# Two layers of attention and quantized feed-forward on one core: the weights' norm factors, the opening and the order of layer 1's attentions rearranged

## The chip, the core and the metric

The kernel runs on one core of a Trainium2 chip. The metric is the device time of one execution in microseconds (us). The engines have these names in the profile: PE (TensorE, matmuls; PEld is its weight load), DVE (VectorE), ACT (ScalarE), POOL (GpSimd), SP (SyncE, which here only issues DMAs).

## What is computed

Eight sequences of 512 tokens with 256 features (B = 8, T = 512, C = 256), each with a context of 512 x 128, 16 heads. Two layers; each adds a gated attention and a gated feed-forward to x:

```python
x = x + tanh(g_xattn[0]) * L0_xattn(layernorm(x), ctx)   # head size 16
x = x + tanh(g_ffn[0])   * L0_ffn(layernorm(x))
x = x + tanh(g_xattn[1]) * L1_xattn(layernorm(x), ctx)   # head size 32
x = x + tanh(g_ffn[1])   * L1_ffn(layernorm(x))

# L0_xattn: causal self-attention plus full cross-attention, one projection
y = softmax(causal(q k')) v + softmax(qc kc') vc;  return y @ Wp + bp
# L0_ffn: both linears on values quantized with ONE scale for all tokens
#   scale = (max(x) - min(x)) / 255, before W1 and, after gelu, before W2
# L1_xattn: two blocks, a1 on (x, x) and a2 on (x, ctx); each block:
xn, yn = ln(x, lnx_g, lnx_b), ln(y, lny_g, lny_b)
a = softmax((xn wq)(yn wk)' / sqrt(32))     # a1: then a *= (t > s)
x_out = x + (a (yn wv)) @ li1 + li1_b
out = x_out + gelu(ln(x_out) @ li2 + li2_b) @ li3 + li3_b
# L1_ffn: ternary weights, activations in 8 bits with a scale per token
h = silu(depthwise_conv1d(bit_linear(x, w1), 3 taps));  return bit_linear(h, w2)
```

The global minimum and maximum after gelu in L0_ffn mean that no second linear of layer 0 can start before the last token's gelu is done. That splits the kernel into two parts.

## The kernel before

A planner at build time (`Pace`) holds a modelled free time for each engine and a modelled ready time for each tile. Work is written as Python generators, *streams*. `weave_timed` (layer 0 and the stage between the layers) and `weave_all` (layer 1) choose, step by step, which stream goes next, and thereby write out the instruction order of every engine; nothing is reordered at run time. A stream yields `need(...)`, the tiles that its next step reads, or `WAIT`. A stream has a base (from which attention on it may run) and a share of the time. All matmuls are issued by `mm` (line 1050) and all transposes by `tp` (line 1053), so rows of PE bear these two lines.

Layer 0, for each sequence b: `norm0` (layer norm), `pre0` (transposes to xnT through `turned_timed`, then `values0`), `pairs0` (the projections Q and K of a half of the heads, self and cross), `cross0` (the cross values), `steps0` (the attention itself: scores into a tile of two PSUM banks, two exponentials, GpSimd's causal mask on the diagonal, then the output matmuls into `ov`), `post0`. PSUM holds three score tiles of two banks (`st`), one bank `ov` and one bank for everything else (`m0`, `bank()`), so that in layer 0 every projection, transpose and value product passes through one bank in turn. Before the first attention stands a chain of norm0(0), pre0(0) and pairs0(0, 0, 0). The weights of layer 1 are loaded and prepared by `load1` beside layer 0's attentions: block a1's during b = 5, a2's during b = 6. Preparing a weight is to multiply the norm's factor into it (line 1542, DVE) and to work the norm's bias through it into a bias of its own (16 small matmuls, or 4 for the values of a1, and a small DVE operation, lines 1529 and 1539).

Between the layers, `layer0_ffn`: `range0(b)` quantizes, multiplies by W1, applies gelu, takes minimum and maximum (tile `hext`, line 1665) and stores the result to DRAM (hd). `keys2` makes the context's keys and values for the first six sequences. Then two reduces into `e` (lines 1589 and 1590) and a chain of small operations give the scale of the second quantization. The PSUM pool here has eight single banks.

Layer 1, `layer1_xattn`: 16 attentions (8 sequences x 2 blocks), each a *slot*, in the order of a list `order`. Slots go in rows: two sequences in a1, the same two in a2, the next two in a1 and so on. The weights li1, li2, li3 of a block are held once, so they are loaded anew for each row: `used` starts the next load when the last sequence of a row has used them, `weight` waits for it. Beside the attentions run these streams:

- `first(b)`: second half of layer 0's feed-forward: loads h (tile hF), on ACT scales and rounds it (line 1912), on DVE clips (1914) and subtracts (1916), and multiplies by W2, in two halves of 256 tokens;
- `pre1`, `pair1`: layer norms, transposes, Q and K of a group of four heads;
- `mlp1(b, blk, half)`: li1, li2, gelu, li3; in its first half for a2 it also loads the sequence's values vt from DRAM;
- `last(b)`: layer 1's feed-forward: the convolution on DVE (line 2290), silu on ACT, the maximum of |h| over 1024 features for each token (hm, line 2298, a reduce), a multiply by the token's scale and the rounding into hq (2315), and the product with w2;
- `tail` for the last sequence, `diagonals`, `keys2_rest`.

An attention slot is four groups of four steps. A step's front is four score matmuls, two exponentials of 128 x 1024 (line 2175) and for a1 the masked diagonal `dg` by GpSimd (line 2179). Its back is the output matmuls and, over the four steps, sums on DVE (lines 2204 and 2206, tile acc); at a group's end ones-matmuls, two DVE transposes, a reciprocal and a multiply (line 2224) give oT and free the one bank of `ov`. PSUM in layer 1: two score tiles of two banks, one bank `ov`, three for the rest.

Of the kernel before, what the change touches and what calls it, by code (L numbers as in the profile page):

```python
# [15 lines left out]
P = 128  # L16
B, T, C, CC = 8, 512, 256, 128
H = 16
NT = T // P
# [7 lines left out]
NEG = -1.0e30  # L27
PTS = 3
# [886 lines left out]
def need(*tiles, pe=True, room=()):  # L915


    return [Pace.name(t) for t in tiles], pe, room
# [30 lines left out]
class Fast(General):  # L949
# [114 lines left out]
    def weave_timed(self, ops, streams, drain=False):  # L1064

        pace, behind = self.pace, self.behind
        ops = list(ops)
        n_ops, i = len(ops), 0  # L1070
        live = list(streams)

        def advance(s):
            w = pace.work
            s.need = next(s.gen, None)
            s.done += pace.work - w
            if s.need is None:
                s.over = True
                if s in live:
                    live.remove(s)  # L1080

        def starts(s):
            names, on_pe, room = s.need
            t = max([pace.when(names)] + [pace.place(tag) for tag in room])
            return max(t, pace.place("m1")) if on_pe else t

        while i < n_ops or live or (drain and not behind.over):
            now = pace.free.get("PE", 0.0)
            cands = []
            for s in live + ([] if behind.over else [behind]):  # L1090
                while s.need is WAIT:
                    last = s.need
                    advance(s)
                    if s.need is WAIT:
                        break
                while not s.over and s.need is not WAIT and not s.need[1] and starts(s) <= now:
                    advance(s)
                if s.over or s.need is WAIT:
                    continue
                cands.append((s.base + s.share * s.done / s.total, starts(s), s))  # L1100
            if i < n_ops:
                cands.append((i / n_ops, ops[i][0](), None))
            if not cands:
                continue
            can = [c for c in cands if c[1] <= now + 0.3]
            pick = min(can, key=lambda c: c[0]) if can else min(cands, key=lambda c: (c[1], c[0]))
            if pick[2] is not None:
                advance(pick[2])
            else:
                ops[i][1]()  # L1110
                i += 1
# [47 lines left out]
    def layer0_xattn(self, w8pool):  # L1159
# [4 lines left out]
        with (  # L1164
# [9 lines left out]
            self.weave_timed([], [Stream(self.chain(self.norm0(0), self.pre0(0), self.pairs0(0, 0, 0)), 1.0)])  # L1174
            for b in range(B):
                streams = [Stream(self.pairs0(b, 1), 7.0, 0.88)]
                if b:
                    streams.append(Stream(self.post0(b - 1), 4.0, 0.88))
                else:
                    streams.insert(0, Stream(self.cross0(0), 5.0, 2.0))  # L1180
                if 1 <= b <= 4:
                    n = ("f0_w1", "f0_w2", "f1_w1", "f1_w2")[b - 1]
                    pool = w8pool if n == "f0_w1" else stage
                    streams.append(Stream(self.few_bits(n, n[1] == "1", pool), 1.0, 0.88))
                if b in (5, 6):
                    streams.append(Stream(self.load1(b - 5), 4.0, 0.88))
                if b + 1 < B:
                    streams.append(Stream(self.norm0(b + 1), 1.0, 0.88))
                streams.append(Stream(self.ctx0(b), 1.0, 0.88))
                self.weave_timed(self.steps0(b, 0), streams)  # L1190
                streams = []
                if b + 1 < B:
                    gen = self.chain(self.pre0(b + 1), self.pairs0(b + 1, 0, 0), self.cross0(b + 1))
                    streams.append(Stream(gen, 14.0, 0.88))
                self.weave_timed(self.steps0(b, 1), streams)
# [154 lines left out]

    def cross0(self, b):
# [18 lines left out]
    def pairs0(self, b, u, *which):  # L1370
# [5 lines left out]
        for s in which or (0, 1):  # L1376
            src = (q["xnT"], q["ctxT"])[s]
            yield need(q["xnT"])
            ps = self.proj(self.wqk[("wq", "wcq")[s]], q["xnT"], u * P)
# [3 lines left out]
            ps = self.proj(self.wqk[("wk", "wck")[s]], src, u * P)  # L1383
# [5 lines left out]
    def steps0(self, b, u):  # L1389
# [7 lines left out]
        def front_at(e, s):  # L1397
            if (u, s) not in q or ("v", s) not in q:
                return 1e9
# [3 lines left out]
        def front(e, s, kt):  # L1403
# [15 lines left out]
            reads = [Pace.name(pt), Pace.name(q["v", s])]  # L1419
            self.coming = (reads, kt == 0, lambda: back(e, s, kt, lo, pt))  # L1420
# [36 lines left out]
        def rest_at():  # L1457
            if self.rest is None:
                return 0.0
            names, opens, _ = self.rest  # L1460
# [40 lines left out]
    def load1(self, blk):  # L1501
# [12 lines left out]
        w = {}  # L1514
        for name, nch, ln in (("wq", 2, "lnx"), ("wk", nchy, "lny"), ("wv", nchy, "lny")):
# [4 lines left out]
            yield need(t)  # L1520
            ps = self.bank()
            if name == "wv" and not blk:
                for c in range(nch):
                    self.mm(
                        ps, self.col(f"{pre}_{ln}_b", c).to_broadcast([P, P]), t[:, c, :],
                        c == 0, c == nch - 1,
                    )
                bias = home.tile([P, 2 * C], F32, name=f"{pre}_{name}_b")
                nc.vector.tensor_copy(bias, ps)
            else:  # L1530
                for g in range(4):
                    for c in range(nch):
                        self.mm(
                            ps[:, g : g + 1], t[:, c, g * P : (g + 1) * P],
                            self.col(f"{pre}_{ln}_b", c), c == 0, c == nch - 1,
                        )
                bias = self.keep2.tile([P, 4], F32, name=f"{pre}_{name}_b")
                s = 32.0 ** -0.5 if name == "wq" else 1.0
                nc.vector.tensor_scalar(bias, ps[:, 0:4], s, None, ALU.mult)
            w[name + "_b"] = bias  # L1540
            for c in range(nch):
                nc.vector.tensor_scalar(
                    t[:, c, :], t[:, c, :], self.col(f"{pre}_{ln}_g", c), None, ALU.mult
                )
        self.w1s.append(w)
        if blk:
# [13 lines left out]
            for p in ("a1", "a2"):  # L1560
                d = self.row1v(f"{p}_li3_b")
                nc.vector.tensor_tensor(d, d, self.row1v(f"{p}_li1_b"), ALU.subtract)

# [4 lines left out]
    def layer0_ffn(self):  # L1568
        nc, tc, small = self.nc, self.tc, self.small
        with (  # L1570
# [10 lines left out]
            for b in range(2):  # L1581
                self.load_cT(b)
            streams = [Stream(self.chain(self.post0(B - 1), self.scales0()), 4.0, 0.01)]
            for b in range(B):
# [152 lines left out]
    def layer1_xattn(self):  # L1737
        nc, tc = self.nc, self.tc
        with (
# [19 lines left out]
            order = [(2 * p + k, blk) for p in range(B // 2) for blk in range(2) for k in range(2)]  # L1759
            few, pairs, mlps, pres = [], [], [[], []], [[], []]  # L1760

            for k, b in zip((-1, 0, 1, 2, 3, 4, 7, 8), range(B)):
# [3 lines left out]
            for k, b in zip((5, 6, 9, 10, 13, 14, 15), range(B - 1)):  # L1766
# [9 lines left out]
            for half in range(2):  # L1776
                mlps[half][-1].base += 0.4 * half
                mlps[half].append(Stream(self.tail(half), 20.0, 1.0, 17 + 0.4 * half))
            self.final, self.tails = {}, [0, 0]
# [4 lines left out]
                [self.steps1(b, blk) for b, blk in order], [few, pairs, *mlps, *pres, diag, keys]  # L1784
# [6 lines left out]
    def weave_all(self, attns, chains):  # L1791
# [14 lines left out]
        def starts(s):  # L1806
            names, on_pe, _ = s.need
            t = max(pace.when(names), pace.free["DVE"] - s.lag)
# [43 lines left out]
    def weight(self, name, b, blk):  # L1852

        while self.loads.get(name) != self.slot_of(b, blk) // 2:
# [3 lines left out]
    def used(self, name, b, blk):  # L1858

        if self.both(b, (name, blk)) and b % 2 and (b, blk) != (B - 1, 1):  # L1860
# [24 lines left out]
    def first(self, b):  # L1885
# [22 lines left out]
        for half in range(2):  # L1908
            if half:
                h = h2 or load_h(1)  # L1910
            yield need(h, pe=False)
            nc.scalar.activation(h, h, AF.Identity, scale=self.rh, bias=self.magic)
            yield need(h, pe=False)
            nc.vector.tensor_scalar(h, h, self.hlo, self.hhi, ALU.max, ALU.min)
            hq = work.tile([P, NF, n], BF16, tag="hq", name="hq")
            nc.vector.tensor_scalar(hq, h, MAGIC, None, ALU.subtract)
# [111 lines left out]
    def slot_of(self, b, blk):  # L2028

        return 4 * (b // 2) + 2 * blk + b % 2  # L2030
# [9 lines left out]
    def pair1(self, b, blk, g):  # L2040
# [17 lines left out]
        self.pairs += 1  # L2058

    def mlp1(self, b, blk, half):  # L2060
# [43 lines left out]
        elif not half:  # L2104
            while self.nvt < self.slot_of(b, 1) or self.backs < 16 * (self.slot_of(b, 1) - 1):
                yield WAIT
            vt = q["vt", 1] = work.tile([P, NT, 2 * C], F32, tag="vt", name="vt", bufs=2)
            self.nvt += 1
            nc.sync.dma_start(vt.rearrange("p t c -> p (t c)"), self.vd[b])
# [134 lines left out]
    def last(self, b):  # L2244
# [25 lines left out]
        for half in range(2):  # L2270
# [3 lines left out]
            for f in range(NF):  # L2274
# [18 lines left out]
            yield need(h, pe=False)  # L2293
            nc.scalar.activation(h, h, AF.Silu)
            yield need(h, pe=False)

            hm = work.tile([P, n], F32, tag="hm", name="hm")
            nc.vector.tensor_reduce(  # L2298
                hm, h.rearrange("p f t -> p t f"), AX.X, ALU.max, apply_absolute_value=True
            )  # L2300
# [11 lines left out]
            yield need(sr, pe=False)  # L2312
            nc.vector.tensor_tensor(h, h, sr.unsqueeze(1).to_broadcast([P, NF, n]), ALU.mult)
            hq = work.tile([P, NF, n], BF16, tag="hq", name="hq")
            nc.vector.tensor_scalar(hq, h, MAGIC, MAGIC, ALU.add, ALU.subtract)
# [239 lines left out]
```

## Time and profile before

| | |
|---|---|
| time, median of 3 runs | 2823.27 us (2820.88 to 2829.08) |
| profiled execution, its own time | 2823.82 us |
| its span | 2822.1 us |
| mean granted TensorE clock | 0.956 |
| PE busy | 2520.0 us (89%) |
| DVE busy | 1725.1 us (61%) |
| ACT busy | 1448.3 us (51%) |
| POOL busy | 615.0 us (22%) |

The span is the profiled execution from its first to its last instruction. Busy times of the engines overlap, and the engine that is busy most is not the only one that sets the end: what counts is what PE waits for, where it waits. "x <- y" in a row of waits means that an instruction on tile x waited for an instruction on tile y. The line numbers are those of the kernel before.

### The profile page before, as it was taken

Reading aid. Unit: us, or ns where it says so; the run is one execution under the profiler, and the core shown is the slowest. Engines: PE = TensorE matmul, PEld = TensorE weight load, DVE = VectorE, ACT = ScalarE, POOL = GpSimd, SP = SyncE. Lnnn points to the kernel's source line nnn. Section 1 sums busy time; section 2 is a strip of 40 time slices with the busy share of each in tenths; the row PEclk is TensorE's granted clock in tenths of the full one; section 3 lists DMA queues with packets and bytes.
Section 4 is the critical chain, followed back from the end, with each engine's and each line's share of the span. In section 5 each row is a group of like instructions: output and inputs, shape, how many; then the busy total and the mean of one; then the engine's idle time right before and its main releaser. Section 6 shows DMA issues by size and latency. Waiting matters only on the chain.

```text
span 2822.1 us, 38446 instructions
## 1 busy us (share of the span) xinstructions
PE 2520.0 (89%) x15452; PEld 1222.3 (43%) x15452; DVE 1725.1 (61%) x3072; ACT 1448.3 (51%) x1785; POOL 615.0 (22%) x682
## 2 busy tenths in 40 slices
PE   6999999999675888999999998999999999898875
PEld 2333333333232334535554445456354455354454
DVE  4544544343475555575657767766767755768766
ACT  4666675666573444445445534454555454555431
POOL 2112222111101343231422121232223112212010
PEclk9999999999897989999999999999999999999988
DMA  3001110010364411312210120131120020121010
GB/s 111 22 29 49 49 64 27 12 34 12 116 272 178 154 45 64 113 64 75 72 53 23 45 90 24 59 131 50 53 90 31 28 78 23 31 83 46 15 45 16
DMA packets 77339, 181.79 MB, mean 64 GB/s; under 512 B 7520, under 2 KB 36576, under 8 KB 69344
## 3 DMA queue, kind: packets, MB, share of 16 engines
q1 hardware_dynamic: 74768, 176.05, 17.9%
q8 instruction: 123, 2.02, 0.3%
q0 software_dynamic: 800, 2.62, 0.3%
q10 hardware_dynamic: 1584, 0.58, 0.1%
q14 instruction: 64, 0.52, 0.1%
HBM read 116.32 MB, written 62.91 MB: 64 GB/s over the span
## 4 chain that ended last, share of the span: by engine, by line
PE 69%; DVE 17%; ACT 7%; issue 3%; POOL 3%; DMA 1%; ACTq 0%; POOLq 0%; DVEq 0%
PE ps L1050 39%; PE ps_s L1050 16%; PE ov L1050 12%; DVE hext L1665 2%; PE ps L1053 2%; POOL dg L2179 1%; ACT pt L1412 1%; ACT pt L2175 1%; DVE hF L2290 1%; DVE hm L2298 1%; DVE acc L2204 1%; DVE mv L1936 1%; DVE acc L2206 1%; DVE rb L2222 1%; ACT hD L2122 1%
## 5 line engine op out<-in xcount | busy, mean ns | idle before, releaser
L2175 ACT ACTIVATE pt<-ps_s 128x1024 f32<-128x1024 f32 x512 | 496.3, 1021 | 443.5 <-PE ps_s L1050 357.1
L1050 PE MATMUL ps_s<-QT,KT 32*128 32x512 f32 (+3 forms) x4096 | 613.2, 610 | 29.0 <-ACT pt L2175 12.6
L1412 ACT ACTIVATE pt<-ps_s 128x1024 f32<-128x1024 f32 (+3 forms) x512 | 411.2, 862 | 197.4 <-PE ps_s L1050 190.9
L1050 PEld LDWEIGHTS ps_s<-QT,KT 32*128 32x128 f32 x4096 | 192.5, 185 | 365.2 <-issue 204.4
L2179 POOL TENSOR_SCALAR_AFFINE_SELECT dg<-pt 128x512 f32<-128x512 f32 x128 | 123.2, 964 | 651.6 <-ACT pt L2175 651.5
L1050 PE MATMUL ps<-li,hD 128*128 128x256 f32 x1024 | 238.8, 389 | 12.1 <-ACT hD L2122 12.1
L1050 PE MATMUL ps<-x3T,li 128*128 128x256 f32 x1024 | 244.0, 390 | 1.4 <-ACT x3T L2092 1.1
L1050 PE MATMUL ov<-pt,v 128*32 128x512 f32 (+3 forms) x2048 | 232.7, 525 | 13.9 <-POOL pt L1415 12.5
L1050 PE MATMUL ov<-pt,vt 128*32 128x512 f32 (+3 forms) x1792 | 204.9, 524 | 39.4 <-DVE oT L2224 33.2
L1050 PEld LDWEIGHTS ps<-li,hD 128*128 128x128 f32 x1024 | 193.4, 193 | 66.2 <-issue 17.6
L1050 PEld LDWEIGHTS ps<-x3T,li 128*128 128x128 f32 x1024 | 192.1, 194 | 55.3 <-issue 15.3
L1415 POOL TENSOR_SCALAR_AFFINE_SELECT pt<-pt 128x512 f32<-128x512 f32 x128 | 87.0, 681 | 477.4 <-ACT pt L1412 477.4
L1942 POOL TENSOR_SCALAR mv<-mv 128x2 f32<-128x2 f32 (+1 forms) x105 | 49.8, 475 | 630.8 <-DVE mv L1937 589.8
L2206 DVE TENSOR_TENSOR acc<-acc,pt 128x2048 f32<-128x2048 f32 x64 | 151.4, 2366 | 8.2 <-ACT pt L2175 7.2
L2204 DVE TENSOR_TENSOR acc<-pt 128x2048 f32<-128x2048 f32 x64 | 149.9, 2342 | 0.6 <-ACT pt L2175 0.6
L1437 DVE STREAM_TRANSPOSE ot<-ov 128x512 f32<-128x512 f32 x64 | 45.8, 716 | 156.3 <-PE ov L1050 156.3
L1050 PE MATMUL ps<-zT,a_wq 128*128 128x512 f32 x256 | 131.7, 640 | 6.1 <-DVE zT L2023 4.1
L2290 DVE SCALAR_TENSOR_TENSOR hF<-hp,cols,hF 128x256 f32<-128x256 f32 x224 | 113.1, 505 | 34.6 <-ACT hF L2281 28.1
L1050 PE MATMUL ps<-li,oT 128*128 128x256 f32 x512 | 128.0, 394 | 1.6 <-DVE oT L2224 1.1
L1050 PEld LDWEIGHTS ps<-li,oT 128*128 128x128 f32 x512 | 94.0, 193 | 44.5 <-issue 16.4
L1050 PEld LDWEIGHTS ov<-pt,v 128*32 128x32 f32 x2048 | 40.5, 107 | 168.0 <-issue 102.2
L1729 ACT ACTIVATE hD<-ps,cols 128x256 f32<-128x256 f32 x121 | 53.7, 472 | 108.8 <-PE ps L1050 72.9
(293 smaller groups left out, 3624.1 us busy)
## 6 DMA issues: line engine op xcount, KB each, us to landing
hd<-h SPq DMA_DIRECT2D x16, 1024.0 KB, 3.9
hF<-hd SPq DMA_DIRECT2D x16, 1024.0 KB, 6.7
li<-in_w_a_dram SPq DMA_DIRECT2D x16, 1024.0 KB, 5.0
fw<-q_f_w SPq DMA_DIRECT2D x22, 512.0 KB, 6.0
xF<-xd SPq DMA_DIRECT2D x22, 512.0 KB, 4.5
kd<-k SPq DMA_DIRECT2D x8, 1024.0 KB, 5.6
vd<-v SPq DMA_DIRECT2D x8, 1024.0 KB, 5.3
res<-rd SPq DMA_DIRECT2D x32, 256.0 KB, 2.7
```

Of the source, the lines that this page charges most:

```text
L1050: self.nc.tensor.matmul(out, lhsT, rhs, start=start, stop=stop, skip_group_check=True)
L1053: self.nc.tensor.transpose(out, in_, self.ident)
L1412: nc.scalar.activation(pt[:, 2 * jp : 2 * jp + 2, lo:], pss[jp][:, :, lo:], AF.Exp)
L1415: nc.gpsimd.affine_select(out=diag, in_=diag, compare_op=ALU.is_ge, fill=0.0, base=0, pattern=[[0, 4], [1, P]], channel_multiplier=-1,)
L1665: nc.vector.tensor_reduce(e, hh, AX.X, op)
L1729: self.nc.scalar.activation(out, ps, AF.Identity, bias=bias)
L1942: nc.gpsimd.tensor_scalar(rstd, mv[:, :, 1], EPS, None, ALU.add)
L2175: nc.scalar.activation(pt[:, 2 * jp : 2 * jp + 2, :], pss[jp], AF.Exp)
L2179: nc.gpsimd.affine_select(out=dg, in_=pt[:, :, diag], compare_op=ALU.is_gt, fill=0.0, base=0, pattern=[[0, 4], [-1, P]], channel_multiplier=1,
L2204: nc.vector.tensor_tensor(st["acc"], st["pt"], pt, ALU.add)
L2206: nc.vector.tensor_tensor(st["acc"], st["acc"], pt, ALU.add)
L2290: nc.vector.scalar_tensor_tensor(a, hp[:, half + k : half + k + n], self.col("conv_w", 3 * f + k), a, ALU.mult, ALU.add)
```

## The change

Four things are changed; the matmuls are the same, in number and shape.

**Opening.** A new `opening0` takes the place of `pre0` and the first `pairs0` for b = 0. All eight transposes go into one score tile of two banks; ACT copies one bank out, DVE the other. Q and K are then projected into the two banks of a second score tile. The values' product moves behind, into a stream beside the first attention, ahead of `cross0`. Fronts of an attention no longer require the values, backs do.

**Norm factors.** The preparation of a1's wq, wk, wv and of a2's wq moves out of `load1` into a new `gains1`, which runs as the stream of the lowest priority in the stage between the layers. Their loads, and all of a2's wk and wv, stay where they were.

**Rows.** Layer 1's attentions go in rows of two, three and three sequences instead of four rows of two. The places from which `first` and `last` may start are shifted to suit, `li` weights are loaded 18 times instead of 24, and the load of vt becomes a stream of its own.

**Halves.** In `first`, the ACT operation and the DVE operations work in two halves of the features. In `last`, the reduce hm goes in two halves of the tokens, and multiply and rounding in two halves of the features. Steps whose first instruction is on ACT are timed by ACT's modelled free time.

```diff
+ROWS = ((0, 1), (2, 3, 4), (5, 6, 7))
+FIRST_AT = (-1, 0, 1, 2, 4, 5, 7, 9)
+LAST_AT = (6, 7, 8, 11, 12, 13, 15)
...
-            self.weave_timed([], [Stream(self.chain(self.norm0(0), self.pre0(0), self.pairs0(0, 0, 0)), 1.0)])
+            self.weave_timed([], [Stream(self.chain(self.norm0(0), self.opening0()), 1.0)])
...
-                    streams.insert(0, Stream(self.cross0(0), 5.0, 2.0))
+                    values = self.values0(0, 0, self.seqs[0]["xnT"], self.wv0["wv"], "bv")
+                    streams.insert(0, Stream(self.chain(values, self.cross0(0)), 12.0, 1.2))
...
+    def opening0(self):
+        q = self.seqs[0]
+        xnT = q["xnT"] = self.work.tile([P, 2, T], F32, tag="xnT", name="xnT", bufs=1)
+        yield need(q["z"], pe=False)
+        ps = self.st.tile([P, 2, T], F32, tag="st", name="ps_s")
+        for c in range(2):
+            for i in range(NT):
+                self.tp(ps[:, c, i * P : (i + 1) * P], q["z"][:, i, c * P : (c + 1) * P])
+        self.nc.scalar.copy(xnT[:, 0, :], ps[:, 0, :])
+        self.nc.vector.tensor_copy(xnT[:, 1, :], ps[:, 1, :])
+        yield from self.pairs0(0, 0, 0, two=True)
...
-            if (u, s) not in q or ("v", s) not in q:
+            if (u, s) not in q:
...
+            n = 2 * C if name == "wv" and not blk else 4
+            w[name + "_b"] = self.keep2.tile([P, n], F32, name=f"{pre}_{name}_b")
+            if home is self.w8pool:
+                yield from self.gains1(blk, name, ln)
...
+            gains = [self.gains1(0, "wq", "lnx"), self.gains1(0, "wk", "lny"), self.gains1(0, "wv", "lny"), self.gains1(1, "wq", "lnx")]
             streams = [Stream(self.chain(self.post0(B - 1), self.scales0()), 4.0, 0.01)]
+            streams.append(Stream(self.chain(*gains), 12.0, 1.0, B))
...
-            order = [(2 * p + k, blk) for p in range(B // 2) for blk in range(2) for k in range(2)]
+            self.rows = [(blk, bs) for bs in ROWS for blk in range(2)]
+            order = self.order = [(b, blk) for blk, bs in self.rows for b in bs]
...
-            for k, b in zip((-1, 0, 1, 2, 3, 4, 7, 8), range(B)):
+            for k, b in zip(FIRST_AT, range(B)):
...
-            for k, b in zip((5, 6, 9, 10, 13, 14, 15), range(B - 1)):
+            for k, b in zip(LAST_AT, range(B - 1)):
...
+            vals = [Stream(self.values2(b), 1.0) for b, blk in order if blk]
...
-            t = max(pace.when(names), pace.free["DVE"] - s.lag)
+            t = max(pace.when(names), pace.free[on] - s.lag)
...
-            yield need(h, pe=False)
-            nc.scalar.activation(h, h, AF.Identity, scale=self.rh, bias=self.magic)
-            yield need(h, pe=False)
-            nc.vector.tensor_scalar(h, h, self.hlo, self.hhi, ALU.max, ALU.min)
+            for f in (slice(0, NF // 2), slice(NF // 2, NF)):
+                yield need(h, pe=False, on="Activation")
+                nc.scalar.activation(h[:, f, :], h[:, f, :], AF.Identity, scale=self.rh, bias=self.magic)
             hq = work.tile([P, NF, n], BF16, tag="hq", name="hq")
-            nc.vector.tensor_scalar(hq, h, MAGIC, None, ALU.subtract)
+            for f in (slice(0, NF // 2), slice(NF // 2, NF)):
+                yield need(h, pe=False)
+                nc.vector.tensor_scalar(h[:, f, :], h[:, f, :], self.hlo, self.hhi, ALU.max, ALU.min)
+                nc.vector.tensor_scalar(hq[:, f, :], h[:, f, :], MAGIC, None, ALU.subtract)
...
-            nc.vector.tensor_reduce(
-                hm, h.rearrange("p f t -> p t f"), AX.X, ALU.max, apply_absolute_value=True
-            )
+            for i in range(2):
+                yield need(h, pe=False)
+                t2 = slice(i * P, (i + 1) * P)
+                nc.vector.tensor_reduce(
+                    hm[:, t2], h[:, :, t2].rearrange("p f t -> p t f"), AX.X, ALU.max, apply_absolute_value=True
+                )
...
-            nc.vector.tensor_tensor(h, h, sr.unsqueeze(1).to_broadcast([P, NF, n]), ALU.mult)
-            nc.vector.tensor_scalar(hq, h, MAGIC, MAGIC, ALU.add, ALU.subtract)
+            for f in (slice(0, NF // 2), slice(NF // 2, NF)):
+                yield need(sr, pe=False)
+                nc.vector.tensor_tensor(
+                    h[:, f, :], h[:, f, :], sr.unsqueeze(1).to_broadcast([P, NF // 2, n]), ALU.mult
+                )
+                nc.vector.tensor_scalar(hq[:, f, :], h[:, f, :], MAGIC, MAGIC, ALU.add, ALU.subtract)
...
```

The body of `gains1` is what stood in `load1`: the bias matmuls into one bank, the bias out of it by DVE, and a DVE multiply by the norm's factor for each chunk of 128 rows.

## The prediction, made before the changed kernel ran

> **What bounds the kernel now.** I read the page's head first, then its chain, then the span by stages, then the waits, then two timelines.
>
> ```profile
> PE 2520.0 (89%) x15452; PEld 1222.3 (43%) x15452; DVE 1725.1 (61%) x3072; ACT 1448.3 (51%) x1785; POOL 615.0 (22%) x682
> PE   6999999999675888999999998999999999898875
> PEclk9999999999897989999999999999999999999988
> PE 69%; DVE 17%; ACT 7%; issue 3%; POOL 3%; DMA 1%; ACTq 0%; POOLq 0%; DVEq 0%
> ```
>
> TensorE is the bound: busy 89% of the span and 69% of the chain that ended last. Its matmuls are the same before and after, so only the 302 us in which it is idle and the stretches at a low granted clock can change. VectorE, 17% of the chain, is what it mostly waits for. The second row has three thin places: the first slice, the slices between the layers, the last two. The stages, cut at those places (span of the stretch, busy PE, PEld, DVE, ACT, POOL, then clock, DMA share, GB/s):
>
> ```profile
> 0.00:31.90 31.90, 13.75 (x41) 7.20 (x42) 16.82 (x82) 6.23 (x11) 9.11 (x10) 1.00 0.55 170
> 31.90:79.10 47.20, 42.49 (x288) 14.28 (x292) 16.97 (x40) 29.36 (x40) 10.04 (x13) 1.00 0.15 51
> 470.60:516.60 46.00, 45.37 (x330) 18.32 (x334) 21.93 (x47) 26.88 (x35) 8.52 (x13) 1.00 0.18 58
> 561.10:606.60 45.50, 44.86 (x334) 18.88 (x338) 20.97 (x47) 27.64 (x35) 8.47 (x12) 1.00 0.16 53
> 874.30:890.00 15.70, 1.54 (x6) 1.21 (x7) 6.91 (x18) 3.15 (x2) 4.53 (x5) 0.50 0.78 267
> 931.00:2663.00 1732.00, 1595.03 (x9746) 832.13 (x9742) 1165.12 (x1965) 844.42 (x974) 437.96 (x446) 0.96 0.18 61
> ```
>
> PE idles 18.2 before the first exponential and 14.2 of the 15.7 between the layers. The two layer-0 stretches in which layer 1's weights are prepared are full (0.6 idle each), so work taken out of them comes off the time. The sixteen attentions of layer 1 leave 137 idle. Who ends those waits (total us, times, longest), from 931 on:
>
> ```profile
> PE ov L1050 <- DVE oT L2224: 33.2, 22, 4.9
> PE ov L1050 <- POOL dg L2179: 19.1, 13, 5.6
> PE ps L1053 <- DVE hm L2298: 16.7, 6, 6.5
> PE ps_s L1050 <- DVE KT L1731: 7.2, 5, 2.2
> PE ps_s L1050 <- ACT KT L1729: 5.8, 5, 1.9
> ```
>
> **Opening.** Timeline of the opening (start, duration, engine, line, operation):
>
> ```profile
> 17.92 3.57 PE L1050 MATMUL ps<-wv_t,xnT 128*128 128x256 f32 x8 [0.67 <-ACT xnT L1319]
> 22.27 1.99 PE L1050 MATMUL ps<-wv_t,xnT 128*128 128x256 f32 x8 [0.78 <-DVE v L1336]
> 25.05 1.98 PE L1050 MATMUL ps<-xnT,wq_p 128*128 128x512 f32 x4 [0.78 <-DVE v L1336]
> 27.81 1.98 PE L1050 MATMUL ps<-xnT,wk_p 128*128 128x512 f32 x4 [0.78 <-ACT QT L1313]
> ```
>
> Here Q starts at 25.05, after both groups of values: 25.05 - 17.92 = 7.1 us leave the path. Q and K get banks of their own: K's wait of 0.8 for the bank goes. Against that, the second chunk is copied by VectorE, which until 18.41 is preparing projection weights; its copy of 0.6-0.7 ends near 19.1 instead of 17.9: +1.2. And what comes first after the transposes runs cold: the same eight matmuls take 3.57 and then 1.99, so Q pays +1.6. That is -5.1. The values' 4.0 us (2 x 1.99) are now in the first attention, which idles 4.7 of its 47.2; I let 2.4 of the 4.0 hide there: **-3.5**, between -6.5 (all hidden, no cold Q) and -1 (nothing hidden).
>
> [...]
>
> **Weights' gains out of layer 0.** Four groups move from there: the bias matmuls of a1's wq, wk, wv and a2's wq, 1.9, 1.9, 2.0 and 1.9 us of PE, 7.7 in all, out of two stretches that are PE-bound. **-6**, between -7.7 and -3 (if the exponentials come to bound these stretches: their lighter neighbours run 41 to 43 us instead of 46, so most of it shows).
>
> **The same gains between the layers.** The new order puts their VectorE work after the last reduces of hext and before the two reduces e. What follows e before:
>
> ```profile
> 865.40 8.87 DVE L1665 TENSOR_REDUCE hext<-h 128x1 f32<-128x2048 f32 x4 [3.87 <-ACT h L1654]
> 874.18 0.16 DVE L1589 TENSOR_REDUCE e<-hext 128x1 f32<-128x16 f32 x1
> 874.54 0.62 SPq L1895 DMA_DIRECT2D hF<-hd  x1
> 882.80 2.09 ACT L1912 ACTIVATE hF<-hF,magic,qh_rs 128x2048 f32<-128x2048 f32 x1 [14.76 <-DMA cT<-cd]
> 884.93 1.35 DVE L1914 TENSOR_SCALAR hF<-hF,qh_lo,qh_hi 128x2048 f32<-128x2048 f32 x1 [6.75 <-DMA cT<-cd]
> 889.65 3.57 PE L1050 MATMUL ps<-fw,hq 128*128 128x256 bf16 x16 [13.79 <-DVE hq L1916]
> ```
>
> VectorE is busy without a gap from 865.4, so nothing covers an insertion: eight multiplies of 0.48 to 0.67, three small biases of 0.16 and a copy of 0.69 are 5.0 to 6.5. The load of hF, issued by SyncE only after e, waits with it, and behind it on SyncE the loads of fw and xF; GpSimd's loads of w and cT likewise. The scale's chain of 3.7 hides in the load's 8.3 as now. PE's own 7.7 run from 866.3 beside the reduces; at half clock they would end near 880 and could hold VectorE a little longer. **+5.3**, between +4.5 and +8. Dequantizing, clipping and subtracting of the first load are now done in halves: ScalarE's 2.09 shows by half, and VectorE's second half alone follows: **-2.7** (0 to -3).
>
> **Rows of two, three, three.** This decides. I laid out both programs' orders of TensorE's instructions and counted, with this trace's durations, how much PE work stands between the producer of an operand and the matmul that uses it. Too little cover is a wait. Output matmuls right behind their sums (the chain of four VectorE operations of 0.72, 0.25, 0.71 and 0.69 us ahead of oT) with under 2.5 us of cover: 20 of 63 before, 16 after. Diagonals from GpSimd under 3 us: 17 of 128, then 11. Keys under 1 us: 11, then 8. Charging the rows above in proportion: 33.2 x 4/20 = 6.6; 19.1 x 6/17 = 6.7; 13.0 x 3/11 = 3.5. The other way, the token maxima (am) with little cover go from 5 to 8 and the quantized inputs of the last feed-forward (xq) from 3 to 6; what such waits cost now is 3.5 us for six (1.9 for am, 1.6 for xq in the same list), 0.6 each, so 3.5 for six more. Sum **-13**. Bounds: half of the 65.3 us of the three rows goes, -33; or each of the four rows of three gets a slot as bad as the worst now (15.2 idle, mean 8.5), +27.
>
> The granted clock falls to 0.50 for 3 to 14 us after longer waits, about 21 times between 931 and 2595. With a tenth of the idle time gone, two of these dips go too, of some 6 us, half of it lost: -6; I take **-4** (-10 to +8). Six loads of li weights fewer: no PE wait in the list is ended by them, 0. The last part, 2663 to 2822, keeps its order, 0 (-8 to +8).
>
> **Halving in layer 1.** 68 more VectorE instructions. The rows give the fixed part: 128x512 takes 0.48, 128x2048 1.30, so 0.53 ns an element and 0.2 us an instruction: 14 us more of VectorE, which is busy 1165 of 1732. In exchange a reduce of 3.7 us that holds up other work becomes two of 1.9. PE shows little of either: **+1**, between -8 (half of hm's 16.7) and +7 (half of the 14).
>
> [...]
>
> **Sum.** The profiled execution took 2823.82 (span 2822.1 and 1.7 around it), 0.55 above the median of 2823.27. -3.5 - 6 + 5.3 - 2.7 - 13 - 4 + 1 = -22.9: **2801**. From no change a measurement of this kernel can tell about 0.3%, 8.5 us.
>
> **Rivals.** *VectorE's queue, slower.* The streams of the last feed-forward now come in threes (slots 6 to 8 and 11 to 13) and the new order gives three slots running 80 to 84 us of VectorE work in about 108. The chain ahead of oT is in the same queue; behind reduces and multiplies of 1.9 to 3.7 us it comes later. If each of the 24 chains of six such slots waits 1.5 us (33.2/22) where 8 do now, that is +24, and with the other parts' -5.9 and no gain in clock +18: 2842. It decides from +14 in the sixteen slots. For it: oT is already the largest wait. Against: the count of short covers falls. Chance 0.2.
>
> *The waits only move.* The sixteen slots keep their 137 idle, with other releasers; opening, layer 0, boundary and halving leave -5.9: 2818, no change that can be told. For it: the covers counted worse. Chance 0.15.
>
> *The clock gains too.* If half of the three rows goes (-33) and with it five dips (-15 for -4), the time is about 2770. Chance 0.07. The forecast has 0.58, on its own 2785 to 2815.
>
> Range: 2778 to 2834, leaving out the outer part of the first rival and of the third. Faster 0.65, same 0.15, slower 0.20.
>
> **What would show it.** First exponential near 27 instead of 31.9; layer-0 stretches of b = 5 and 6 shorter by 3 each; the reduces e near 870 (874.2 - 9.5 + 5.3), and the first dequantization 8 us behind; waits of ov for oT near 27 and for dg near 12; idle in the sixteen slots near 125. I am wrong if the slots' idle time rises, or if VectorE's oT rows grow.

## The result and the profile after

The changed kernel takes 2781.72 us, median of 4 runs (2781.44 to 2786.96), against 2823.33 for the kernel before beside it: ratio 0.9854, 95% interval 0.9835 to 0.9873. That is 41.6 us less; 22.9 were forecast. The time lies inside the range, 3.7 us above its lower end, and below the 2785 to 2815 that the forecast itself was given. The profiled execution has a span of 2779.7, 42.4 less than before.

The head of the page of the changed kernel:

```profile
PE 2517.8 (91%) x15447; PEld 1223.8 (44%) x15452; DVE 1736.5 (62%) x3135; ACT 1452.2 (52%) x1803; POOL 614.8 (22%) x682
PE   7999999999786989999999999988999989999875
PEclk9999999999886999999999999999999999999987
```

The same matmuls, almost the same busy time (2.2 us less), a span shorter by 42.4: nearly all of it came out of PE's idle stretches. The stages of the changed kernel, cut as before (span, busy PE, PEld, DVE, ACT, POOL, clock, DMA share, GB/s), with its last part added:

```profile
0.00:28.80 28.80, 13.82 (x32) 5.92 (x32) 16.96 (x82) 5.62 (x10) 9.10 (x10) 1.00 0.60 189
28.80:76.40 47.60, 44.32 (x296) 15.47 (x300) 17.20 (x42) 28.98 (x38) 10.23 (x13) 1.00 0.15 50
468.00:509.60 41.60, 39.92 (x294) 14.13 (x290) 19.26 (x39) 26.42 (x34) 8.36 (x13) 1.00 0.18 58
554.10:599.20 45.10, 43.66 (x318) 17.25 (x322) 20.37 (x45) 26.95 (x34) 7.98 (x12) 1.00 0.14 48
923.00:2610.80 1687.80, 1578.81 (x9734) 826.27 (x9732) 1165.43 (x1993) 847.66 (x994) 440.33 (x446) 0.97 0.18 59
2610.80:2779.70 168.90, 113.40 (x500) 83.25 (x498) 113.65 (x237) 44.93 (x75) 11.63 (x19) 0.80 0.08 26
```

The sixteen attentions of layer 1 idle 109 instead of 137, and run 1687.8 instead of 1732; the last part is 10 longer, 7.6 of it PE work that moved there. The two traces stage by stage, each stage from the stamps of its first and last instructions:

| stretch | before | after | difference | predicted |
|---|---|---|---|---|
| to the first exponential | 31.9 | 28.8 | -3.1 | with the next row -3.5 |
| first attention | 47.2 | 47.6 | +0.4 | |
| rest of layer 0's attentions | 648.0 | 643.0 | -5.0 | -6 |
| from there to the reduces e | 147.1 | 152.5 | +5.4 | +5.3 |
| e to the first matmul on hq | 15.5 | 11.6 | -3.9 | -2.7 |
| from there to layer 1's first exponential | 41.6 | 39.5 | -2.1 | 0 |
| sixteen attentions and last part | 1890.8 | 1856.7 | -34.1 | -16 |

Every step but the last two is within 1.2 us of its term. Layer 1 gave twice what was charged, and the experiments are about that. Its waits in the changed kernel, from its first exponential at 923 on (total us, times, longest; other rows left out):

```profile
PE ov L1053 <- DVE oT L2266: 29.4, 18, 4.9
PE ps L1056 <- DVE z L144: 17.7, 18, 3.0
...
PE ps L1056 <- DVE hm L2342: 9.7, 6, 3.2
PE ps_s L1053 <- DVE KT L1761: 7.7, 5, 2.2
...
PE ov L1053 <- POOL dg L2221: 7.1, 10, 1.6
```

The waits on the diagonals dg fell from 19.1 to 7.1, those on hm from 16.7 to 9.7 (a reduce of 3.71 us became two of 1.92, but see rows_alone below), those on oT from 33.2 to 29.4. Waits on keys (KT, from VectorE and ScalarE together) fell from 13.0 to 10.3. Waits on layer norms (z) rose from 12.9 to 17.7.

### The profile page after: what moved, and what is told of

Same layout as the page of the kernel before. It is cut to its first block, busy times and chain, and to the rows that moved or that the text cites. A ratio compares the mean times of both kernels' runs of the same rounds, so it can differ in the third digit from the quotient of the medians.

```text
span 2779.7 us, 38478 instructions
## 1 busy us (share of the span) xinstructions
PE 2517.8 (91%) x15447; PEld 1223.8 (44%) x15452; DVE 1736.5 (62%) x3135; ACT 1452.2 (52%) x1803; POOL 614.8 (22%) x682
## 4 chain that ended last, share of the span: by engine, by line
PE 46%; DVE 13%; ACT 4%; POOL 2%; issue 2%; DMA 0%; ACTq 0%; POOLq 0%; DVEq 0%; SPq 0%
PE ps L1053 31%; PE ps_s L1053 8%; PE ov L1053 6%; ACT pt L2217 2%; PE ps L1056 1%; DVE hF L2332 1%; DVE acc L2246 1%; POOL dg L2221 1%; DVE rb L2264 1%; DVE hm L2342 1%; DVE z L144 1%; DVE mv L1971 1%; DVE rt L2261 1%; DVE oT L2266 1%; DVE acc L2248 1%
## 5 line engine op out<-in xcount | busy, mean ns | idle before, releaser
L1053 PE MATMUL ps_s<-QT,KT 32*128 32x512 f32 (+3 forms) x4096 | 613.2, 607 | 28.3 <-ACT pt L2217 16.1
L1053 PE MATMUL ov<-pt,vt 128*32 128x512 f32 (+3 forms) x1792 | 204.4, 526 | 36.2 <-DVE oT L2266 29.4
L1977 POOL TENSOR_SCALAR mv<-mv 128x2 f32<-128x2 f32 (+1 forms) x105 | 57.7, 550 | 770.4 <-DVE mv L1972 735.3
L2221 POOL TENSOR_SCALAR_AFFINE_SELECT dg<-pt 128x512 f32<-128x512 f32 x128 | 116.1, 908 | 505.6 <-ACT pt L2217 505.4
L1053 PEld LDWEIGHTS ps<-li,oT 128*128 128x128 f32 x512 | 92.9, 191 | 47.7 <-issue 16.1
```

Of the source, the lines that this page charges most:

```text
L1053: self.nc.tensor.matmul(out, lhsT, rhs, start=start, stop=stop, skip_group_check=True)
L1977: nc.gpsimd.tensor_scalar(rstd, mv[:, :, 1], EPS, None, ALU.add)
L2221: nc.gpsimd.affine_select(out=dg, in_=pt[:, :, diag], compare_op=ALU.is_gt, fill=0.0, base=0, pattern=[[0, 4], [-1, P]], channel_multiplier=1,
```

## Experiments

Each kernel ran beside the kernel before; ratios are to that. "Layer 1" is the time of one profiled execution from layer 1's first exponential to the end: 1890.8 before, 1856.7 after. Four executions of one kernel scatter by 2 to 14 us. Three kernels whose TensorE order in layer 1 is the same (the changed kernel, early_state and late_open below) have 1856.7, 1853.9 and 1861.8, so a difference under 8 us between two single profiles is not read unless a second profile or the times agree with it.

**Rows undone, halves undone, and each alone.** The edits against the changed kernel (pairs, whole):

```diff
# pairs
-ROWS = ((0, 1), (2, 3, 4), (5, 6, 7))
-FIRST_AT = (-1, 0, 1, 2, 4, 5, 7, 9)
-LAST_AT = (6, 7, 8, 11, 12, 13, 15)
+ROWS = ((0, 1), (2, 3), (4, 5), (6, 7))
+FIRST_AT = (-1, 0, 1, 2, 3, 4, 7, 8)
+LAST_AT = (5, 6, 9, 10, 13, 14, 15)
# whole: first() and last() as in the kernel before
# rows_alone, halves_alone: these parts of the change put into the kernel before
```

> The changed kernel with layer 1's attentions in rows of two again and the starting places of first and last as before; opening, norm factors and halves stay changed. From the first exponential of layer 1 to the end the kernel before took 1890.8 us, the changed one 1856.7. Theory 1, the order of rows gives those 34 us: this kernel loses at least 25 of them, about 2810. Theory 2, the halves give them (a 3.7 us reduce no longer blocks VectorE's queue): it keeps at least 25, at most 2790. Theory 3, they only come together, or by the planner's luck: something between, and rows alone and halves alone do not add up.

Measured: 2800.06, ratio 0.9910 (0.9893 to 0.9926); layer 1 1877.1.

> The changed kernel with first and last working in whole pieces again (and their steps timed by VectorE's free time). Theory 1 (rows): layer 1 stays within 8 us of the changed kernel; the start of layer 1 is later by about 3.5 (the first dequantization again in one piece), so about 2785. Theory 2 (halves): layer 1 gives back 25 or more, about 2810. By the prediction's own terms it would be 2782 + 2.7 - 1 = 2784.

Measured: 2775.50, ratio 0.9832 (0.9811 to 0.9853); layer 1 1848.7.

> The kernel before with nothing changed but the rows of two, three, three, the starting places and the stream for vt. Theory 1 (rows): layer 1 shorter by 25 to 34, about 2793. Theory 2 (halves): within 8 of the kernel before. The prediction charged it -17 (13 of idle time, 4 of clock), 2806.

Measured: 2809.12, ratio 0.9938 (0.9922 to 0.9955); layer 1 1872.7.

> The kernel before with nothing changed but the halves in first and last. Theory 1 (rows): 2820, that is -3.5 at the start of layer 1 and nothing in it. Theory 2 (halves): layer 1 shorter by 25 or more, about 2795. The prediction charged it -2.7 + 1, 2822.

Measured: 2820.88, ratio 0.9985 (0.9976 to 0.9995); layer 1 1887.0.

The rows, with their places, are worth 16 to 18 us, alone (2825.5 - 2809.1) as well as inside the change (0.9910 against 0.9854): what the prediction charged for order and clock, 17. Theory 2 falls: halves alone are worth 4.6, about what the trace shows at the start of layer 1, and taken out of the changed kernel they cost nothing (0.9832 against 0.9854, the intervals overlap). The rows have their worth by other waits than the prediction counted. From rows_alone:

```profile
PE ov L1053 <- DVE oT L2236: 31.2, 20, 4.9
PE ov L1053 <- POOL dg L2191: 17.8, 13, 5.7
PE ps L1056 <- DVE hm L2310: 6.9, 3, 3.6
```

Against the kernel before, oT fell by 2.0 and dg by 1.3; hm fell by 9.8, with the reduce still in one piece. But theory 1 doesn't suffice either: rows alone leave layer 1 at 1872.7, and the kernel without halves, whose generators in layer 1 are the same as those of rows alone, needs 1848.7. 24 us came from something that no part of the change says it does in layer 1.

**Where the rest is: the state in which the planner enters layer 1.**

```diff
# gains_early, against the changed kernel
-            if home is self.w8pool:
-                yield from self.gains1(blk, name, ln)
+            yield from self.gains1(blk, name, ln)
...
-            streams.append(Stream(self.chain(*gains), 12.0, 1.0, B))
# pairs_whole: pairs and whole together
```

> The changed kernel with all norm factors worked in beside layer 0's attentions again. By the changed kernel's trace the move gave 5 us in layer 0 and cost 5.4 between the layers, so on its own it is worth nothing, and this kernel takes about 2782. But rows alone left layer 1 at 1872.7 us from its first exponential, and the changed kernel without halves, the same streams of layer 1, at 1848.7: what else differs is the state in which the planner enters layer 1. If the moved factors make that state, layer 1 of this kernel falls back to 1870 or more, and the time is about 2797.

Measured: 2795.08, ratio 0.9887 (0.9870 to 0.9903); layer 1 1868.2.

> The changed kernel with rows of two and with whole pieces in first and last: opening, norm factors and the stream for vt are all that is left of the change. If the state in which the planner enters layer 1 shortens any order, layer 1 is near 1870 here, and the time near 2795. If that state only suits rows of three, layer 1 stays within 6 of the 1890.8 of the kernel before, and the time is near 2816.

Measured: 2811.26, ratio 0.9949 (0.9932 to 0.9965); layer 1 1884.1. Between the two expectations: rows of two gain 7 us in layer 1 from the entry.

So moving the norm factors is worth 9 to 13 us (by the ratios, whose intervals just touch, and by the medians). Its direct effects nearly cancel: -5.0 and +5.4 against the kernel before, and 843.1 instead of 845.2 from the first exponential to the reduces e against gains_early, which shares the opening. With the factors late, the planner has spent 4.75 us more of PE's modelled time after the last stores of h, and so it believes ScalarE, SyncE, GpSimd and the wires to be free 4.75 earlier, relative to PE, and hF to land earlier, than without. It writes out another order: in the two traces, PE's first 52 instructions after the reduces e are the same, and the 53rd is another. That can be tried without moving any work:

```diff
# early_state: gains_early, and before_state: the kernel before, each with this at the entry to layer 1
+            for e in ("Activation", "SP", "Pool"):
+                self.pace.free[e] += -4.75
+            self.pace.wire += -4.75
```

> All norm factors beside layer 0's attentions, as in gains_early (2795.1; layer 1 1868.2 from its first exponential), with one more edit in the planner alone: at the entry to layer 1 its modelled free times of ScalarE, SyncE, GpSimd and of the wires are set back by 4.75 us, which is what they differ by there between the changed kernel and gains_early. TensorE's order in layer 1 is then the changed kernel's, matmul for matmul. If moving the norm factors paid only through this state, layer 1 is near 1857 and the start of it a little earlier too, and the time near 2782. If it is the work itself that has to stand there, it stays near 2795.

Measured: 2785.63 (2775.46 to 2789.62), ratio 0.9862 (0.9846 to 0.9879); layer 1 1853.9, in a profiled execution of 2775.46, the shortest of its four by 9.5.

> The kernel before, and nothing changed but the same 4.75 us in the planner's model at the entry to layer 1. If the state is worth by itself what it was worth in pairs_whole (layer 1 1884 instead of 1891, its start 4 earlier after the reduces e), about 2812; if it needs the moved work, 2824.

Measured: 2813.57, ratio 0.9955 (0.9938 to 0.9971); layer 1 1883.8, its start 3.4 earlier after the reduces e (53.8 us behind them instead of 57.1).

Three lines that touch nothing but the planner's model gain 11.6 us on the kernel before. On gains_early they gain 9.5 by the medians and 7 by the ratios; those intervals overlap, but each of the four executions is below each of gains_early's. That brings it within 4 us of the changed kernel, with overlapping intervals. PE's order in layer 1 is that of pairs_whole in before_state, and the two profiles agree (1884.1 and 1883.8). The first four attentions of gains_early and then of early_state, same columns as above:

```profile
926.70:1327.30 400.60, 370.09 (x2225) 180.67 (x2224) 231.17 (x365) 191.19 (x217) 124.50 (x119) 0.95 0.20 69
```

```profile
919.80:1305.70 385.90, 360.14 (x2225) 176.72 (x2224) 234.10 (x373) 186.47 (x210) 127.15 (x119) 0.97 0.21 72
```

2225 matmuls in both; 14.7 us between them. Idle time is 4.7 of it (30.5 against 25.8), and the other 10 are PE's own busy time, at a granted clock of 0.97 instead of 0.95. The changed kernel and late_open, with early_state's order, need 386.4 and 385.7 here: against gains_early 6.6 to 6.8 us less idle and 7.4 to 8.3 less busy. In the kernel before and then before_state it is almost all idle time, 11.3 of 12.2:

```profile
931.30:1332.20 400.90, 366.35 (x2257) 180.90 (x2256) 237.08 (x367) 189.62 (x205) 128.92 (x120) 0.95 0.23 78
```

```profile
928.80:1317.50 388.70, 365.45 (x2255) 182.91 (x2254) 233.19 (x357) 194.03 (x217) 133.79 (x120) 0.97 0.24 80
```

The waits of ov for oT fall there from 11.1 to 3.0, those for dg from 11.1 to 6.3. So the planner's state works above all on these first four attentions: they take 394 to 401 us in all four kernels that enter layer 1 with the old state (factors early, model not shifted) and 379 to 390 in all ten that enter it with a shifted one. How much of the gain is busy time differs from order to order.

**Rows with the old places.**

```diff
# old_places, against the changed kernel
-FIRST_AT = (-1, 0, 1, 2, 4, 5, 7, 9)
-LAST_AT = (6, 7, 8, 11, 12, 13, 15)
+FIRST_AT = (-1, 0, 1, 2, 3, 4, 7, 8)
+LAST_AT = (5, 6, 9, 10, 13, 14, 15)
```

> The changed kernel with rows of two, three, three, but with the places from which first and last may start as they were before. If the rows themselves shorten layer 1 (fewer changes between a1 and a2), it stays within 6 us of 2781.7. If it is the later places of last, which spread VectorE's heavy streams, it loses 10 or more of the 18 between the changed kernel and the one in pairs, 2792 or above.

Measured: 2831.17, ratio 1.0022 (1.0013 to 1.0032); layer 1 1906.3: 50 us lost, more than any part of the change gains. The sixth to eighth attentions lose 30.9 of them, with 247 us of VectorE work in three attentions instead of 221; the ninth and tenth win 14.3 back, and the eleventh and twelfth lose 24.7. Its twelfth attention, and that of the changed kernel below it:

```profile
2109.10:2243.30 134.20, 114.64 (x729) 62.57 (x731) 101.41 (x171) 60.72 (x72) 32.74 (x36) 0.95 0.07 24
```

```profile
2077.30:2198.50 121.20, 112.24 (x718) 61.26 (x714) 91.41 (x173) 57.55 (x70) 46.14 (x52) 0.99 0.21 69
```

VectorE has 101 us of work in one attention, and PE idles 19.6 instead of 9.0. Its eleventh and twelfth attentions together hold 8 multiplies and 8 roundings of `last` and 6 halves of hm, 27.1 us, where the changed kernel has 4, 4 and 4, 16.1 us, beside nearly the same convolution rows (48 and 46): the ends of several `last` streams come together. In the twelfth, PE's waits that VectorE ends are 10.9 us, against 3.1 in the changed kernel. That is VectorE's queue, as in the prediction's slower rival, but not by the rival's way: it had priced the chains ahead of oT, and the waits of ov for oT in layer 1 are 25.0 here, fewer than in the changed kernel (29.4). The lists of starting places keep it away; both lists were put back at once, so the share of `first` and of `last` stays open. Whether rows of two would also gain from other places wasn't tried, so 16 to 18 us is the worth of rows and places together.

**A better version.** The trace of the changed kernel shows two costs that the change brought. VectorE's part of the norm factors stands before e, and hF's load waits for it:

```profile
858.19 8.87 DVE L1695 TENSOR_REDUCE hext<-h 128x1 f32<-128x2048 f32 x4 [4.05 <-ACT h L1684]
867.63 3.41 PE L1053 MATMUL ps<-cols,a_wq 128*128 128x1 f32 x16
871.15 0.88 DVE L1588 TENSOR_SCALAR a_wq<-a_wq,cols 128x512 f32<-128x512 f32 x2
871.94 0.16 DVE L1619 TENSOR_REDUCE e<-hext 128x1 f32<-128x16 f32 x1
880.59 2.37 ACT L1946 ACTIVATE hF<-hF,magic,qh_rs 128x1024 f32<-128x1024 f32 x2 [19.39 <-DMA cT<-cd]
```

And in the opening K still waits 0.78 for QT to be copied out, since the two banks are one tile:

```profile
16.83 4.22 PE L1053 MATMUL ps_s<-xnT,wq_p 128*128 128x512 f32 x4 [0.68 <-ACT xnT L1365]
21.83 3.78 PE L1053 MATMUL ps_s<-xnT,wk_p 128*128 128x512 f32 x4 [0.78 <-ACT QT L1317]
```

```diff
# late_open, against the changed kernel; rest() is the DVE part of gains1
             nc.vector.tensor_reduce(e[:, 1:2], self.hext[:, 1, :], AX.X, ALU.min)
+            for rest in self.late[:3]:
+                rest()
             sh, self.rh, self.hlo, self.hhi = self.affine_scale(e, "qh")
+            for rest in self.late[3:]:
+                rest()
...
-        self.nc.vector.tensor_copy(xnT[:, 1, :], ps[:, 1, :])
+        self.nc.scalar.copy(xnT[:, 1, :], ps[:, 1, :])
...
+            banks = self.st.tile([P, 2, T], F32, tag="st", name="ps_s") if two else None
             ps = self.proj(self.wqk[("wk", "wck")[s]], src, u * P, ps=two and banks[:, 1, :] or None)
# whole_late: the same with first() and last() of the kernel before
# late_state: whole_late with 1.09 us taken off all modelled times but TensorE's at the entry to layer 1
```

> The changed kernel with two edits: VectorE's part of the norm factors is put behind the two reduces e (three weights before the scale's chain, the fourth after it), and in the opening both chunks are copied by ScalarE and K gets a score tile of its own. TensorE's order in layer 1 is the same as in the changed kernel. If the 5.4 us stood in front of hF's load and nothing else, they now hide in the load: hF's first rounding 4.8 earlier, first exponential 1.2 earlier, 2776 in all. If the load is late for another reason (the wires, or SyncE's queue), 2781.

Measured: 2774.86, ratio 0.9821 (0.9803 to 0.9839), an interval that overlaps the changed kernel's. The profile of late_open:

```profile
852.20 8.87 DVE L1710 TENSOR_REDUCE hext<-h 128x1 f32<-128x2048 f32 x4 [3.86 <-ACT h L1699]
860.98 0.16 DVE L1630 TENSOR_REDUCE e<-hext 128x1 f32<-128x16 f32 x1
861.35 0.62 SPq L1943 DMA_DIRECT2D hF<-hd  x1
867.85 0.87 DVE L1593 TENSOR_SCALAR a_wq<-a_wq,cols 128x512 f32<-128x512 f32 x2
869.43 2.37 ACT L1961 ACTIVATE hF<-hF,magic,qh_rs 128x1024 f32<-128x1024 f32 x2 [14.58 <-DMA hF<-hd]
```

From the first of the last four reduces to the first rounding it is 17.2 instead of 22.4: 5.2 us, and the multiplies now run while the load is under way. The place was the cost, not the work. In the opening K's matmuls follow Q's without a wait; what that is worth can't be told, since the same opening scatters by more (see below).

> As late_open, and first and last work in whole pieces: the best parts together. If the parts add up, 2775.5 - 6 = 2769.5. TensorE's order in layer 1 differs from that of the kernel with whole pieces from its 44th matmul on; if that order is luck, it can be 10 more or less.

Measured: 2772.60, ratio 0.9812 (0.9796 to 0.9828).

> whole_late (2772.6) with the planner's model at the entry to layer 1 set back by 1.09 us on all engines but TensorE, which restores the order of the kernel with whole pieces (2775.5) in layer 1. If that order is better than whole_late's by the 5 to 10 us that their profiles differ by in layer 1, 2765; if those were scatter of single executions, 2772.

Measured: 2767.73 (2763.84 to 2778.08), ratio 0.9802 (0.9776 to 0.9827). Between the two expectations, and its ratio lies inside the interval of whole_late: whether this order of layer 1 is the better one stays open. It has the lowest median of all, 57 us under the kernel before.

## Why the prediction was right, and what it missed

The time fell inside the range, with 18.7 us more gained than forecast. 9 to 13 of these came from an effect that the prediction had at nothing, the planner's state; the others are of the size of the scatter and are not assigned.

**Opening** (-3.5, measured -2.7). The direction and nearly the size in this pair of executions, by the wrong items. Q started at 16.83, not 19.1, because its first half needs only the chunk that ScalarE copies. The wait for the bank did not go. And both Q and K took longer, 4.22 and 3.78 against 1.98 each in the kernel before: the prediction charged 1.6 for one. In the profile of old_places, with the same opening, Q took 3.44 and K 1.98. The traces' first record of the granted clock, at full, comes 12.8 us after the first matmul here, when K was through, and 6.5 us in old_places, before K began; what sets that moment these runs do not show. Over all profiles, the old opening took 31.9 to 34.1 us to the first exponential (four kernels) and the new one 26.0 to 28.8 (seven), so the pair compared lies at the low end of its worth.

**Gains out of layer 0** (-6, measured -5.0). Sized rightly in sum, not in its places: 4.4 at b = 5, where three of the four weights were, and 0.4 at b = 6, where "shorter by 3 each" had been said.

**Gains between the layers** (+5.3, measured +5.4), as worked out. That late_open takes it back by moving only VectorE's part shows the cause. **Halves at the start** (-2.7, measured -3.9).

**Rows** (-13 of idle time and -4 of clock). The rows' own worth, 16 to 18, is what was charged, but largely by luck: the count of cover had the wrong waits. By rows_alone oT fell by 2.0 where 6.6 had been charged, dg by 1.3 instead of 6.7, keys by 0.3 instead of 3.5; layer 1 still lost 10.5 us of idle time and 7.7 of PE's busy time, because waits fell that had not been charged: hm by 9.8, z by 8.2 (after VectorE and ScalarE together), hD by 4.1, against 4.0 more on the exponentials pt. The falls of dg and oT in the changed kernel came with the planner's state and the halves: dg is 14.3 in before_state and 11.4 in halves_alone.

**What failed** is the charge for the norm factors, -6 and +5.3 and nothing in layer 1. The step "the gains between the layers" followed VectorE, SyncE and GpSimd at run time, but not the planner at build time: the moved work changes its modelled times, these change the order, and the state alone is worth 11.6 us on the kernel before and 7 to 9.5 on gains_early. In layer 1 it is worth 7 us in the kernel before, 11 to 14 against gains_early, and rows_alone and whole are 24.0 apart, so the parts of the change do not simply add up to the 34.1. Of these, 25.8 are idle time and 8.3 PE's busy time.

**Halving in layer 1** (+1). The term was right to be near nothing for the time, and its 14 us of VectorE were right too: VectorE's busy time in the whole profile is 1738.4 in halves_alone against 1725.1 (77 more instructions), and 1736.5 in the changed kernel against 1720.1 in whole (84 more), 0.17 and 0.20 us an instruction. PE showed little of it. In rows of two with the later state halves gain 11 (0.9949 against 0.9910), in the kernel before 4.6, with rows of three nothing that can be told: their worth depends on the order.

**The rivals.** The slower one did not come: VectorE's work reached 83 to 92 us in five of the attentions, more than the rival's 80 to 84, and oT still fell. That VectorE's queue can cost is shown by the old starting places, 50 us, though by other waits than oT. The waits did not merely move: the sixteen attentions idle 109 us instead of 137. The third, about 2770, lies nearer to the measured 2781.7 than the forecast's 2801; its way, half of the waits for oT, dg and keys gone, was half true: they fell by 18.5, not 33. Of the dips of the granted clock to 0.50 in the sixteen attentions 4 of 21 went, where the forecast had two and the rival five.

## What to carry to other kernels

When a planner writes the order, a moved piece of work has a second effect, through the model's state, that no trace of before shows: separate it by shifting the model alone, and try such shifts before crediting an edit with a gain. Place heavy streams by counting the busiest helper engine's work in each window: with the old starting places for VectorE's streams, rows of three lost 50 us, more than any edit gained. A count of covers that comes out at the right sum is not yet right: undo each part alone and read which waits went. Work put into a gap pays if it stands behind the instruction that starts the transfer which fills the gap: here that was 5.2 us.

## What the runs showed of the hardware

The same opening took 26.0 to 28.8 us to the first exponential in seven kernels that share it, and PE's busy time in it was 10.9 to 13.8. The traces show what goes with it: in four of them the granted clock is first recorded, at full, at 25.6 to 26.2 us, and K's four matmuls, begun before, took 3.64 to 3.78 us; in the other three it is recorded at 19.9 to 20.3, and K's took 1.98. So K's four matmuls stand ahead of the clock's first record in some executions of the same opening instructions and behind it in others, and ahead of it they took 1.66 to 1.80 us longer.

Two orders of the same matmuls can differ in PE's busy time as well as in its idle time: 14.7 us apart, of which 4.7 were idle time, in one pair; 12.2 apart, of which 11.3 were idle time, in another; the granted clock was 0.95 against 0.97 in both. There is no fixed rate between them in these runs.
